# Attention weights of a two-layer graph network moved from SBUF to PSUM for VectorE's products

## The chip, the cores and the metric

The kernel runs on one core of one Trainium2 chip. The core has TensorE (PE in the profile, its weight loads PEld), VectorE (DVE), ScalarE (ACT), GpSimd (POOL) and SyncE (SP), which run beside each other and meet at semaphores; SBUF and PSUM are its on-chip memories, PSUM in 8 banks. The metric is the device time of one execution in microseconds: the median of the timed runs.

## The reference

Two graph layers run over x of shape (8, 2048, 256) with one adjacency matrix of 2048 x 2048, which has about 9 edges in a row. Layer 0 is chunked attention, layer 1 a graph attention with leaky-ReLU logits. Both end in a residual sum and a layer norm.

```
# layer 0: softmax within each chunk of 256 columns, masked entries count as score -10
q, k, v = heads(x @ Wq.T + bq), heads(x @ Wk.T + bk), heads(x @ Wv.T + bv)        # 4 heads of 64
scores = where(mask == 0, -10, clip(q.k / 8, -10, 10))                             # per chunk
ctx = sum over chunks of softmax(scores) @ v
x = layernorm(x + layernorm(ctx @ Wo.T + bo + x) * gamma + beta)              # eps 1e-5
# layer 1
Wh = x @ W
e = leaky_relu(s_src[i] + s_dst[j], 0.2), where adj, else -inf
x = layernorm(x + elu(softmax(e) @ Wh))
```

## The kernel before

The kernel works on edge lists rather than on dense matrices. A first part (`edge_lists`) reads the adjacency matrix, finds up to 24 neighbours of each row, and sorts the rows by how many they have, into 16 tiles of 128 rows; tile t takes `CAPS[t]` neighbour slots, 24 for the first and 5 for the last. A dense path exists for adjacency matrices that don't fit and isn't taken.

Layer 0 runs in 4 groups of 2 batches, so in 64 steps (g, t). The tables of keys and values (`kv_d`) and of queries and residuals (`qx_d`) of a group are written to DRAM by `tables`, one tile per step, one group ahead. A step then does the following. `fetch0` gathers, for each neighbour slot, 128 rows of `kv_d` with one indirect DMA on GpSimd's queue (L489) into a unit of two slots; the units come from a ring of 14 buffers. `scores0` multiplies keys by queries on VectorE (L547 into another buffer, L554 in place). For most units PE then transposes the products (L566), ScalarE copies them (`prT`, L572) and PE sums over the head's elements with a selection matrix (L576), so that the scores land in a PSUM bank; for the other units VectorE reduces (L556). `softmax0` reads the scores (L590) and makes the weights `al` (L596 to L607). `context0` multiplies the values by the weights: three quarters of the units on VectorE in one instruction each (`weighted`, L501, with the weights broadcast over 64 elements), the last quarter on ScalarE, 64 elements at a time (`weighted_act`, L507). PE transposes and accumulates the products in a bank "acc" (`summed`, L514). `finish0` is the output projection and both layer norms; `rows1` transposes its rows (`transposed`, L307), copies them (`x1T`, L658), projects them (L663) and writes the table `wh_d` of layer 1.

Layer 1 runs in 2 halves of 4 batches, so in 32 steps (p, t): `fetch1` gathers from `wh_d`, `softmax1` adds the logits (L680) and makes the weights `e` (to L700), `context1` multiplies and accumulates as in layer 0, `finish1` makes the norm, and scatters (L748, L753) put rows back in order through GpSimd's queue. The first half is interleaved with the layer-0 steps of groups 2 and 3; the second half runs alone at the end. Gathers are called one step ahead. On each engine the instructions stand in an order that the tile framework's scheduler made from the program's order; a buffer or bank is reused when its last reader is done.

PSUM has 8 banks: two each of "tf" (scores of layer 0 and the transposed rows of `rows1`), "tk" (the tables' transposes and projections), "acc", and one each of "mf" and "pr".

Of the kernel before, what the change touches and what calls it, by code (L numbers as in the profile page):

```python
# [14 lines left out]
ALU = mybir.AluOpType  # L15
AX = mybir.AxisListType

P = 128
# [16 lines left out]
TOP = 24  # L35
REC = 32
G = 2
UNIT = 2
# [135 lines left out]
def sparse_path(ctx: ExitStack, tc: tile.TileContext, keep, x, adj, Wq, bq, Wk, bk, Wv, bv, Wo, bo, gamma, beta, W, a,  # L174
                out):
    nc = tc.nc
# [5 lines left out]
    GF = G * F  # L182
    GH = G * H
# [46 lines left out]
    ps = ctx.enter_context(tc.tile_pool(name="ps", bufs=2, space=bass.MemoryType.PSUM))  # L230

    def bank(tag, bufs=2):

        return ps.tile([P, 512], F32, tag=tag, name=tag, bufs=bufs)

    with tc.tile_pool(name="prep", bufs=2) as prep:
        for dst, w, scale in ((wq, Wq, 0.125), (wkv[:, :, 0:F], Wk, 1.0), (wkv[:, :, F:], Wv, -1.0 / CH), (wo, Wo, 1.0)):
            wn = prep.tile([P, KC, F], F32, tag="wn", name="wn")
            nc.scalar.dma_start(wn, w.rearrange("(c p) f -> p c f", p=P))
            pt = bank("mf", 1).rearrange("p (c f) -> p c f", c=KC)  # L240
# [277 lines left out]
    got0, st0 = {}, {}  # L518
# [12 lines left out]
    def scores0(g, t):  # L531
        S = CAPS[t]
        qx, units = got0[g, t]
        q = qx[:, 0:GF]
        sc = small.tile([P, GH, S], F32, tag="sc", name="sc")

        npe = 1 + len(units) - len(units) // 3
        ps_sc = bank("tf")[:, 0:GH * S].rearrange("p (s e) -> p s e", e=GH)
        W8 = GH * DP
        qv = q.rearrange("p (k j w) -> p k j w", k=UNIT, w=W8).unsqueeze(3)  # L540

        def product(i):

            u, s0, n = units[i]
            room = units[i - 1][0][:, :, 0:GF]
            prod = room.rearrange("p k (j w) -> p k j w", w=UNIT * W8)[:, :, :, 0:n * W8]
            nc.vector.tensor_tensor(prod.rearrange("p k j (s w) -> p k j s w", w=W8),  # L547
                                    u[:, :, 0:GF].rearrange("p s (k j w) -> p k j s w", k=UNIT, w=W8),
                                    qv.to_broadcast([P, UNIT, NJ // UNIT, n, W8]), op=ALU.mult)
            return prod  # L550

        def reduced(u, s0, n):
            prod = u[:, :, 0:GF].rearrange("p s (j w) -> p s j w", w=W8)
            nc.vector.tensor_tensor(prod, prod, q.rearrange("p (j w) -> p j w", w=W8).unsqueeze(1)  # L554
                                    .to_broadcast([P, n, NJ, W8]), op=ALU.mult)
            nc.vector.tensor_reduce(sc[:, :, s0:s0 + n].rearrange("p e s -> p s e"),  # L556
                                    prod.rearrange("p s j (e d) -> p s e j d", d=DP),
                                    axis=AX.XY, op=ALU.add)
        reduced(*units[0])
        for i in range(1, npe, 4):  # L560
            some = units[i:min(i + 4, npe)]
            pr = bank("pr", 1).rearrange("p (k r) -> p k r", r=P)
            for k, (u, s0, n) in enumerate(some):
                prod = product(i + k)
                for j in range(NJ):
                    nc.tensor.matmul(pr[0:n * W8, k, :], prod[:, j // (NJ // UNIT), j % (NJ // UNIT), :], ident, is_transpose=True,  # L566
                                     start=(j == 0), stop=(j == NJ - 1), skip_group_check=True)
            m = len(some)
            prT = work.tile([P, 4, P], F32, tag="prT", name="prT", bufs=1)
            full = m - 1 if some[-1][2] < UNIT else m  # L570
            if full:
                nc.scalar.copy(prT[:, 0:full, :], pr[:, 0:full, :])  # L572
            if full < m:
                nc.scalar.copy(prT[0:W8, full, :], pr[0:W8, full, :])
            for k, (u, s0, n) in enumerate(some):
                nc.tensor.matmul(ps_sc[:, s0:s0 + n, :], prT[0:n * W8, k, :], sel[0:n * W8, 0:n * GH],  # L576
                                 start=(s0 == UNIT), stop=(k == m - 1 and i + m == npe), skip_group_check=True)
        for unit in units[npe:]:
            reduced(*unit)
        st0[g, t] = ps_sc, sc, min(S, UNIT * npe)  # L580


    ebuf = const.tile([P, GH * TOP + 1], F32, name="ebuf")
# [2 lines left out]
    def softmax0(g, t):  # L586
        S = CAPS[t]
        n = GH * S
        ps_sc, sc, sp = st0.pop((g, t))
        nc.vector.tensor_scalar(sc[:, :, UNIT:sp], ps_sc[:, UNIT:sp, :].rearrange("p s e -> p e s"), -10.0, 10.0, op0=ALU.max,  # L590
                                op1=ALU.min)
        for some in [sc[:, :, 0:UNIT]] + ([sc[:, :, sp:]] if sp < S else []):
            nc.vector.tensor_scalar(some, some, -10.0, 10.0, op0=ALU.max, op1=ALU.min)
        e = ebuf[:, 0:n]
        ev = e.rearrange("p (e s) -> p e s", s=S)
        nc.scalar.activation(ev, sc, AF.Exp)  # L596
        nc.vector.scalar_tensor_tensor(ev, ev, -EMIN, valid[:, t, 0:S].unsqueeze(1).to_broadcast([P, GH, S]),
                                       op0=ALU.add, op1=ALU.mult)

        al = small.tile([P, GH, S], F32, tag="al", name="al")  # L600
        z = al.rearrange("p e s -> p (e s)")
        nc.vector.tensor_tensor_scan(z, same[t][:, 0:n], e, 0.0, op0=ALU.mult, op1=ALU.add)
        zb = small.tile([P, n], F32, tag="zb", name="zb", bufs=1)
        nc.vector.tensor_tensor_scan(zb[:, ::-1], ebuf[:, n:0:-1], same[t][:, n:0:-1], 0.0, op0=ALU.add, op1=ALU.mult)
        nc.vector.scalar_tensor_tensor(z, z, CH * EMIN, zb, op0=ALU.add, op1=ALU.add)
        nc.vector.reciprocal(z, z)
        nc.vector.tensor_tensor(al, al, ev, op=ALU.mult)  # L607
        st0[g, t] = al

    def context0(g, t):  # L610
        S = CAPS[t]
        al = st0.pop((g, t))
        units = got0[g, t][1]
        acc = bank("acc").rearrange("p (c r) -> p c r", r=P)

        na = len(units) // 4
        if g == PG:
            places(t, units)
        for u, s0, n in units[len(units) - na:]:
            weighted_act(u[:, :, GF:2 * GF], al, s0, n)  # L620
        for i, (u, s0, n) in enumerate(units):
            if i < len(units) - na:
                weighted(u[:, :, GF:2 * GF], al, s0, n)
            summed(acc, u[:, :, GF:2 * GF], s0 == 0, s0 + n == S)
        cT = work.tile([P, G * KC, P], F32, tag="cT", name="cT", bufs=1)
        nc.scalar.copy(cT, acc)
        st0[g, t] = cT
# [25 lines left out]
    def rows1(g, t):  # L653

        o = st0.pop((g, t))
        pt = transposed(o.rearrange("p b f -> p (b f)"), "tf", 2)
        xT = work.tile([P, G * KC, P], F32, tag="x1T", name="x1T", bufs=1)
        nc.scalar.copy(xT, pt)  # L658
        wh = work.tile([P, WW], F32, tag="whs", name="whs")
        for b in range(G):  # L660
            pw = bank("mf", 1)
            for kc in range(KC):
                nc.tensor.matmul(pw[:, 0:F + 2 * H], xT[:, b * KC + kc, :], wa[:, kc, :], start=(kc == 0), stop=(kc == KC - 1))  # L663
            nc.scalar.copy(wh[:, b * F:(b + 1) * F], pw[:, 0:F])
            nc.scalar.copy(sd[g // 2 % 2][:, t, g % 2, b * H:(b + 1) * H], pw[:, F:F + H])
            nc.scalar.copy(wh[:, GF + b * H:GF + (b + 1) * H], pw[:, F + H:F + 2 * H])  # L666
        nc.sync.dma_start(wh_d[g // 2][t * P:(t + 1) * P, g % 2 * WW:(g % 2 + 1) * WW], wh)
# [7 lines left out]
    def softmax1(p, t):  # L675
# [21 lines left out]

        nc.vector.tensor_scalar(r, r, 1e-30, None, op0=ALU.max)
        nc.vector.reciprocal(r, r)
        nc.vector.tensor_tensor(e, e, r.unsqueeze(2).to_broadcast([P, 2 * GH, S]), op=ALU.mult)  # L700
        st1[p, t] = e

    def context1(p, t):
        S = CAPS[t]
        e = st1.pop((p, t))
        units = got1.pop((p, t))
        accs = [bank("acc").rearrange("p (c r) -> p c r", r=P) for _ in range(2)]
        na = len(units) // 4, (len(units) + 2) // 4
        for i, (u, s0, n) in enumerate(units):
            for k in range(2):  # L710
                if i >= len(units) - na[k]:
                    weighted_act(u[:, :, k * WW:k * WW + GF], e[:, k * GH:(k + 1) * GH], s0, n)
        for i, (u, s0, n) in enumerate(units):
            for k in range(2):
                part = u[:, :, k * WW:k * WW + GF]
                if i < len(units) - na[k]:
                    weighted(part, e[:, k * GH:(k + 1) * GH], s0, n)
                summed(accs[k], part, s0 == 0, s0 + n == S)
        hTs = []
        for k in range(2):  # L720
            hT = work.tile([P, G * KC, P], F32, tag="hT", name="hT")
            nc.scalar.copy(hT, accs[k])
            hTs.append(hT)
        xr = work.tile([P, 2, GF], F32, tag="xr", name="xr")
        nc.sync.dma_start(xr, x1_d[p][t * P:(t + 1) * P])
        st1[p, t] = hTs, xr
# [560 lines left out]
```

## Time and profile before

| | us |
|---|---|
| timed runs, median of 3 | 2586.16 (2584.35 to 2596.95) |
| profiled execution, its own time | 2397.55 |
| its span | 2395.8 |
| busy in the span: PE / DVE / POOL / ACT | 1900.4 / 1833.5 / 1505.0 / 1409.0 |
| 984 gathers L489: from kv_d, from wh_d (mean of one) | 810.2 (1.235), 416.5 (1.270) |
| 546 weighted products L501: layer 0, layer 1 (mean of one) | 334.5 (1.234), 314.4 (1.212) |

Busy time is what the engine spent in instructions; issuing and waiting don't count. A line of the groups view gives line, engine, operation, output and inputs with their shapes, the number of instructions, busy time and mean ns of one, and the idle time just before them with what ended it. In a waits view each line gives who waited for whom, the total, how many times, and the longest. The granted TensorE clock was 0.885 of full speed on the mean.

### The profile page before, as it was taken

Reading aid. Unit: us, or ns where it says so; the run is one execution under the profiler, and the core shown is the slowest. Engines: PE = TensorE matmul, PEld = TensorE weight load, DVE = VectorE, ACT = ScalarE, POOL = GpSimd, SP = SyncE. Lnnn points to the kernel's source line nnn. Section 1 sums busy time; section 2 is a strip of 40 time slices with the busy share of each in tenths; the row PEclk is TensorE's granted clock in tenths of the full one; section 3 lists DMA queues with packets and bytes.
Section 4 is the critical chain, followed back from the end, with each engine's and each line's share of the span. In section 5 each row is a group of like instructions: output and inputs, shape, how many; then the busy total and the mean of one; then the engine's idle time right before and its main releaser. Section 6 shows DMA issues by size and latency. Waiting matters only on the chain. (4 is left out here: it accounts for less than half of the span.)

```text
span 2395.8 us, 38844 instructions
## 1 busy us (share of the span) xinstructions
PE 1900.4 (79%) x11946; PEld 1622.0 (68%) x11946; DVE 1833.5 (77%) x4099; ACT 1409.0 (59%) x5036; POOL 1505.0 (63%) x1230
## 2 busy tenths in 40 slices
PE   7686889889899898999988885888678786664764
PEld 5565677778778787777876774776566675554653
DVE  6864587877588988588988886887788887775775
ACT  4573455546566555655565665664356677665766
POOL 3125455672666676376668856774677685787883
PEclk9897899899999999999998997987878987877887
DMA  7737877795889798598879977896679896786884
GB/s 259 242 137 272 265 270 281 260 346 209 316 287 320 260 334 319 212 388 298 302 258 353 360 281 238 285 321 221 230 274 326 306 319 248 278 310 231 302 296 154
DMA packets 239982, 669.10 MB, mean 279 GB/s; under 512 B 43688, under 2 KB 70059, under 8 KB 237719
## 3 DMA queue, kind: packets, MB, share of 16 engines
q0 software_dynamic: 156800, 505.01, 60.1%
q1 hardware_dynamic: 79248, 151.55, 17.2%
q10 hardware_dynamic: 3718, 9.97, 1.3%
q8 instruction: 98, 1.61, 0.3%
q14 instruction: 118, 0.96, 0.1%
HBM read 612.79 MB, written 126.36 MB: 309 GB/s over the span
## 5 line engine op out<-in xcount | busy, mean ns | idle before, releaser
L489 POOL DMA_INDIRECT u<-kv_d,idx x656 | 810.2, 1235 | 436.4 <-PE acc L514 185.7
L514 PE MATMUL acc<-ident,u 128*128 128x128 f32 x5248 | 713.4, 291 | 157.0 <-DVE u L501 89.0
L514 PEld LDWEIGHTS acc<-ident,u 128*128 128x128 f32 x5248 | 637.5, 151 | 220.7 <-DVE u L501 133.2
L489 POOL DMA_INDIRECT u<-wh_d,idx x328 | 416.5, 1270 | 148.2 <-issue 76.4
L566 PE MATMUL pr<-ident,u 128*128 128x128 f32 (+1 forms) x1984 | 287.0, 295 | 78.7 <-DVE u L547 77.2
L501 DVE TENSOR_TENSOR u<-u,al 128x1024 f32<-128x1024 f32 x280 | 334.5, 1234 | 1.5
L566 PEld LDWEIGHTS pr<-ident,u 128*128 128x128 f32 (+1 forms) x1984 | 245.4, 151 | 110.8 <-DVE u L547 104.6
L547 DVE TENSOR_TENSOR u<-u,qx 128x1024 f32<-128x1024 f32 (+1 forms) x248 | 302.0, 1218 | 18.3 <-DMA u<-kv_d,idx 15.1
L501 DVE TENSOR_TENSOR u<-u,z 128x1024 f32<-128x1024 f32 x266 | 314.4, 1212 | 0.6
L507 ACT ACTIVATE u<-u,z 128x64 f32<-128x64 f32 x1008 | 262.0, 337 | 25.0 <-DVE z L700 17.1
L507 ACT ACTIVATE u<-u,al 128x64 f32<-128x64 f32 x800 | 209.1, 342 | 23.2 <-DVE al L607 22.3
L663 PE MATMUL mf<-wa,x1T 128*128 128x264 f32 x512 | 167.6, 455 | 23.1 <-ACT x1T L658 14.8
L351 POOL TENSOR_TENSOR xt<-xt,beta_r 128x1024 f32<-128x1024 f32 x32 | 77.1, 2410 | 143.1 <-PE tk L336 126.3
L385 PE MATMUL tk<-wq,xT 128*128 128x256 f32 x512 | 145.2, 397 | 24.4 <-ACT kvs L379 24.4
L451 ACT ACTIVATE nm<-sums 128x2 f32<-128x2 f32 (+1 forms) x160 | 32.4, 202 | 221.3 <-DVE sums L641 122.6
L372 PE MATMUL tk<-wkv,xT 128*128 128x256 f32 x512 | 151.7, 410 | 12.9 <-ACT xC L341 12.6
L635 PE MATMUL mf<-wo,cT 128*128 128x256 f32 x512 | 148.4, 415 | 6.3 <-ACT whs L666 5.3
L376 PE MATMUL tk<-wkv,xC 128*128 128x256 f32 x512 | 144.5, 399 | 0.0
L663 PEld LDWEIGHTS mf<-wa,x1T 128*128 128x128 f32 x512 | 101.7, 218 | 59.7 <-ACT x1T L658 23.6
L455 ACT ACTIVATE sq<-o,nm 128x256 bf16<-128x256 f32 x256 | 129.7, 507 | 5.3
L554 DVE TENSOR_TENSOR u<-u,qx 128x1024 f32<-128x1024 f32 (+1 forms) x96 | 116.0, 1214 | 16.6 <-DMA qx<-qx_d,node 7.1
L590 DVE TENSOR_SCALAR sc<-tf 128x64 f32<-128x64 f32 (+5 forms) x64 | 14.0, 218 | 138.2 <-PE tf L576 138.2
(168 smaller groups left out, 3254.0 us busy)
## 6 DMA issues: line engine op xcount, KB each, us to landing
kv_d<-kvs SPq DMA_DIRECT2D x48, 512.0 KB, 6.0
wh_d<-whs SPq DMA_DIRECT2D x64, 260.0 KB, 5.8
xt<-in_x_dram SPq DMA_DIRECT2D x64, 256.0 KB, 4.8
qx_d<-xt SPq DMA_DIRECT2D x32, 512.0 KB, 4.4
qx_d<-qs SPq DMA_DIRECT2D x64, 256.0 KB, 5.8
x_d<-o SPq DMA_DIRECT2D x64, 256.0 KB, 5.2
xr<-x_d SPq DMA_DIRECT2D x32, 512.0 KB, 4.9
u<-kv_d,idx POOLq DMA_INDIRECT x656, 6.5
```

The lines of the kernel that those rows point to most:

```text
L372: nc.tensor.matmul(pm[:, 0:F], xT[:, b * KC + kc, rows], wkv[:, kc, 0:F], start=(kc == 0), stop=False, skip_group_check=True)
L376: nc.tensor.matmul(pm[:, F:], xC[:, b * KC + kc, rows], wkv[:, kc, F:], start=False, stop=(kc == KC - 1), skip_group_check=True)
L385: nc.tensor.matmul(qb, xT[:, b * KC + kc, rows], wq[:, kc, :], start=(b == 0 and kc == 0), stop=False, skip_group_check=True)
L455: nc.scalar.activation(sq, src[:, k, :], AF.Square, bias=nm[:, k:k + 1], accum_out=m2[:, k:k + 1])
L489: nc.gpsimd.indirect_dma_start(out=u[:, k, 0:width], out_offset=None, in_=table, in_offset=bass.IndirectOffsetOnAxis(ap=idx[:, t, s0 + k:s ...
L501: nc.vector.tensor_tensor(pv, pv, av, op=ALU.mult)
L507: nc.scalar.activation(pe, pe, AF.Copy, scale=al[:, e, s0 + k:s0 + k + 1])
L514: nc.tensor.matmul(acc[:, c, :], part[:, k, c * P:(c + 1) * P], ident, is_transpose=True, start=first and k == 0 and c == 0, stop=last and ...
L547: nc.vector.tensor_tensor(prod.rearrange("p k j (s w) -> p k j s w", w=W8), u[:, :, 0:GF].rearrange("p s (k j w) -> p k j s w", k=UNIT, w=W8),
L566: nc.tensor.matmul(pr[0:n * W8, k, :], prod[:, j // (NJ // UNIT), j % (NJ // UNIT), :], ident, is_transpose=True, start=(j == 0), stop=(j ...
L635: nc.tensor.matmul(po[:, b, :], cT[:, b * KC + kc, :], wo[:, kc, :], start=(b == 0 and kc == 0), stop=False, skip_group_check=True)
L663: nc.tensor.matmul(pw[:, 0:F + 2 * H], xT[:, b * KC + kc, :], wa[:, kc, :], start=(kc == 0), stop=(kc == KC - 1))
```

## The change

The weights that VectorE multiplies by now lie in PSUM. In layer 0 the score bank gets a tag of its own, "sc", with one buffer: columns up to 192 hold the scores, the columns behind them the weights `w`. In layer 1 the weights go to a bank "e1", with one buffer. ScalarE's products still read SBUF: for the units that it takes (the last quarter), a second, short product puts the weights into `al` or `e` as before. The bank "tf" is gone; the row transposes of `rows1` take their banks from "tk". The sum of banks stays 8. Products of keys and queries are as they were.

```diff
@@ scores0
-        ps_sc = bank("tf")[:, 0:GH * S].rearrange("p (s e) -> p s e", e=GH)
+        scb = bank("sc", 1)
+        ps_sc = scb[:, 0:GH * S].rearrange("p (s e) -> p s e", e=GH)
...
-        st0[g, t] = ps_sc, sc, min(S, UNIT * npe)
+        st0[g, t] = scb, sc, min(S, UNIT * npe)
@@ softmax0
-        ps_sc, sc, sp = st0.pop((g, t))
+        scb, sc, sp = st0.pop((g, t))
+        ps_sc = scb[:, 0:n].rearrange("p (s e) -> p s e", e=GH)
...
-        nc.vector.tensor_tensor(al, al, ev, op=ALU.mult)
-        st0[g, t] = al
+        w = scb[:, GH * TOP:GH * TOP + n].rearrange("p (e s) -> p e s", s=S)
+        nc.vector.tensor_tensor(w, al, ev, op=ALU.mult)
+
+        first = len(got0[g, t][1]) - len(got0[g, t][1]) // 4
+        if UNIT * first < S:
+            nc.vector.tensor_tensor(al[:, :, UNIT * first:], al[:, :, UNIT * first:], ev[:, :, UNIT * first:], op=ALU.mult)
+        st0[g, t] = w, al
@@ context0
-        al = st0.pop((g, t))
+        w, al = st0.pop((g, t))
...
-                weighted(u[:, :, GF:2 * GF], al, s0, n)
+                weighted(u[:, :, GF:2 * GF], w, s0, n)
@@ rows1
-        pt = transposed(o.rearrange("p b f -> p (b f)"), "tf", 2)
+        pt = transposed(o.rearrange("p b f -> p (b f)"), "tk", 2)
@@ softmax1
-        nc.vector.tensor_tensor(e, e, r.unsqueeze(2).to_broadcast([P, 2 * GH, S]), op=ALU.mult)
-        st1[p, t] = e
+        w = bank("e1", 1)[:, 0:2 * GH * S].rearrange("p (e s) -> p e s", s=S)
+        nc.vector.tensor_tensor(w, e, r.unsqueeze(2).to_broadcast([P, 2 * GH, S]), op=ALU.mult)
+        first = len(units) - (len(units) + 2) // 4
+        if UNIT * first < S:
+            nc.vector.tensor_tensor(e[:, :, UNIT * first:], e[:, :, UNIT * first:],
+                                    r.unsqueeze(2).to_broadcast([P, 2 * GH, S - UNIT * first]), op=ALU.mult)
+        st1[p, t] = w, e
@@ context1
-        e = st1.pop((p, t))
+        w, e = st1.pop((p, t))
...
-                    weighted(part, e[:, k * GH:(k + 1) * GH], s0, n)
+                    weighted(part, w[:, k * GH:(k + 1) * GH], s0, n)
```

## The prediction

> **What bounds the kernel now.** I read the page's busy table first, then busy time by stage, then what each engine waited for in each stage, then groups and timeline. The busy table alone names no bound:
>
> ```profile
> PE 1900.4 (79%) x11946; PEld 1622.0 (68%) x11946; DVE 1833.5 (77%) x4099; ACT 1409.0 (59%) x5036; POOL 1505.0 (63%) x1230
> ...
> 330.00:1100.00 770.00, 692.32 (x4427) 592.62 (x4426) 599.95 (x1196) 437.57 (x1677) 471.29 (x373) 0.95 0.82 293
> 1100.00:2010.00 910.00, 727.17 (x4721) 628.30 (x4719) 747.30 (x1612) 542.36 (x2000) 628.62 (x488) 0.87 0.82 289
> 2010.00:2396.00 386.00, 230.48 (x1557) 197.13 (x1555) 263.45 (x636) 257.57 (x906) 277.89 (x225) 0.80 0.73 266
> ```
>
> The last three lines are stages (length, then PE, PEld, DVE, ACT, POOL busy, granted clock, DMA share, GB/s). From 330 to 1100 us layer 0 runs alone, and PE is busy 90%. From 1100 to 2010 both layers interleave, and DVE leads (82%). From 2010 the second half of layer 1 runs alone (the tail). There POOL only looks 72% busy: each of its operations has some 0.30 us of issue time before it that isn't booked as busy (31.7 us over 104, below), 225 x 0.30 = 68 us, so it is taken 346 of 386 us. What ends waits in the tail agrees:
>
> ```profile
> DVE z L680 <- DMA u<-wh_d,idx: 63.6, 27, 5.0
> ...
> POOL u L489 <- issue: 31.7, 104, 0.3
> POOL out_dram L753 <- ACT xr L470: 27.9, 8, 13.4
> POOL u L489 <- PE acc L514: 6.4, 21, 0.3
> ```
>
> (us in total, times, longest.) DVE waits for gathers, while POOL waits hardly for ring buffers, only for its scatters' data (28 us). So **the tail is bound by POOL's issuing of gathers**; earlier stages aren't: in 330-1100 and 1100-2010 POOL itself waits 86.7 and 96.4 us for PE to free ring buffers.
>
> What sets the price of one gather is in the timeline:
>
> ```profile
> 1227.45 2.35 DVE L501 TENSOR_TENSOR u<-u,al 128x1024 f32<-128x1024 f32 x2
> ...
> 1227.66 1.89 POOL L489 DMA_INDIRECT u<-kv_d,idx  x1
> ...
> 1232.22 1.00 POOL L489 DMA_INDIRECT u<-kv_d,idx  x1 [0.30 <-PE acc L514]
> ```
>
> A gather issued while a weighted product (L501) runs takes 1.89 us, one that meets none 1.00. Sorted by the DVE instruction running at its start, the 984 gathers show: beside none 1.00 us (256 of them); beside the reduction L556, which reads one tensor, 1.00 (52); beside L641, whose one input is in PSUM, 1.00 (27); beside the products L501, L547, L554, which read two SBUF tensors, 1.69 (206), 1.44 (153), 1.47 (48).
>
> [...]
>
> ```profile
> L738 DVE SCALAR_TENSOR_TENSOR xr<-mf,xr 128x512 f32<-128x512 f32 x64 | 43.8, 684 | 21.5 <-ACT hT L737 9.9 <-DMA xr<-x_d 7.5 <-SPq L868 4.1
> L547 DVE TENSOR_TENSOR u<-u,qx 128x512 f32<-128x512 f32 x20 | 13.6, 679 | 0.1
> ```
>
> With one input in PSUM 684 ns, with both in SBUF 679. [...]
>
> **The change part by part**, against the profiled execution's own 2397.55 us (span 2395.8 and 1.8 around it). The median of the timed runs, 2586.16, is 189 us longer, for a reason that the profile doesn't show; I carry the sum over as microseconds, not as a share.
>
> *Weights read from PSUM (L501, 546 products).* Gathers beside them should fall to 1.00 us. Each indirect DMA's time above 0.995 us, shared out by overlap, sums to 277 us, of which beside L501: 2 us before 330, 21 in 330-1100, 67 in 1100-2010, 41 in the tail: 132 in all. L547 and L554 keep their share. What of it counts: in the tail POOL's 346 us becomes 305, but its scatters wait for ACT's rows, and these grow as POOL arrives earlier: between 20 and 41 us, I take 30. In 1100-2010 late gathers hold DVE 16.8 + 6.5 = 23 us, so up to 23; I take half, 12. In 330-1100 DVE waits 12 us for gathers and PE is full: 3. Sum -45, from -25 to -75. DVE gains too[...]: the 1024-element L501 means 1242 and 1216 ns (276 and 264 of them) against its undisturbed 1211, 10 us: -10.
>
> *Price of the PSUM operand.* By L738 at most 5 ns each, 3 us[...]. I take 0[...]. The writes of the weights (L607, L700) are as long as before. No row shows a DVE write into PSUM[...].
>
> *Copies of the tail weights for ACT.* 56 extra products in layer 0 (none where a step has three units), 32 in layer 1, 8 to 48 elements, by L680 and L698 (213 and 196 ns) 0.2 us each: 18 us of DVE. The 72 ahead of the tail, 14 us, lie where DVE is 78-82% busy: +11. ACT's products (L507) wait for them 0.2 us longer; ACT is 59% busy, so nothing, and without that cover 18 us more.
>
> *One bank "sc" for scores and weights.* PE may write step k+1's scores (L576) only when step k's last DVE product has read its weight. In the trace of before this always holds: over 63 steps the first score matmul starts 1.9 to 41 us after it. In the built program's PE order, too, they stand behind all of step k's accumulation matmuls (L514), in the changed kernel as in this one. 0; if that cover went, eight score matmuls (1.06 us) and a prT copy (0.58), some 1.6 us a step. Queued behind a waiting L576 on PE would be the table matmuls, and DVE's L590.
>
> *One bank "e1".* The next weights are written 1.1 us or more after the last product read the old ones, both on DVE: 0, either way.
>
> *Row transposes in the tables' banks.* They leave "tf" and become a fifth user per step of two "tk" banks (2 key/value, 1 query, 2 of x every second step). PE waits for tk evacuations today 24.4 (L385), 12.6 (L372) and 11.6 us (L336), 49 in all; a quarter more users, a quarter more: +12. Bounds -5 (the scores no longer share with the rows) and +69 (the rival below). Queued behind such a wait on PE are the products' transposes L566, hence L576 and DVE's L590. On POOL, add_beta (L351) waits for the x transposes and holds gathers; after 330 us that was 20 us, once. Neither SP's nor POOL's list of instructions changes in number.
>
> *Order.* The scheduler reshuffles DVE and PE: more of step k+1's products stand inside step k's softmax, more lies ahead of L590. That cuts L590's 138 us of waiting and delays weights: both signs, 0, with +-20.
>
> Sum: -45 - 10 + 11 + 12 = -32 us.
>
> **Rivals.** *Slower, the tk banks.* A row transposition holds a tk bank for four transposes (0.6 us) and the ACT copy (0.58 us), plus ACT's delay (22.4 us over 64, 0.35): 1.5 us. Tables and rows share the banks in about 46 steps up to 1425 us, where PE is 90% busy and waits for nothing cheaply: 69 us at most. From 44 us (two thirds exposed) on it eats the gain of 45 + 10 - 11. For it: the tk waits of up to 10.9 us at L385. Against: ACT is under 60% busy there. At its full price it gives -45 - 10 + 11 + 69 = +25, 2611.
>
> *Larger gain.* POOL's 132 us all count, because gathers that land earlier let the ring turn faster. For: POOL with its issue time is at 85% in 1100-2010. Against: there it waits 96 us for the ring. -132 - 10 + 11 + 12 = -119, 2467.
>
> *Nothing.* A gather is also held by something else (DMA at 0.82 busy)[...]: the tail keeps its time, within 13 us. Against: the 1.00 us beside L641 and only 0.73 DMA share in the tail.
>
> **How the numbers follow.** Forecast, -32: 2554 (own range 2525 to 2573), 0.45. Larger gain, 2467 (2445 to 2525): 0.15. Nothing, 2586 (2573 to 2599): 0.17. Slower, 2611 (2599 to 2645, with the reshuffle's 20 against it): 0.23. About 0.5%, 13 us, is what a measurement can tell from no change. So faster 0.60, same 0.17, slower 0.23. The range 2490 to 2615 leaves out some 0.09 of the larger gain and 0.10 of the slower case.
>
> **What would show it.** Gathers beside weighted products at 1.00 us, the mean of wh_d gathers from 1270 to about 1130 ns, kv_d from 1235 to about 1170; the tail from 386 to about 356 us; DVE's wait for gathers in the tail well under 64 us; 88 short products more; the weighted product still 1.21 us. Wrong if gathers beside them stay at 1.69 us[...],[...] if waits of tk or L590 grow by over 40 us (banks), or if gathers quicken and the tail does not (then POOL wasn't the bound).

## The result, and the profile after

The changed kernel takes **2713.73 us** (median of 4 runs, 2710.95 to 2725.14) beside 2585.26 us for the kernel before (4 runs, 2567.22 to 2596.95): a ratio of **1.0512** [1.0443, 1.058], slower by 128 us. The prediction was 2554 us, faster by 32.

The same kernel runs at two speeds, and a session (kernels run one after the other on one chip) is here wholly of one kind or the other. In three sessions the kernel before took 2384 to 2390 us; in two, and in the comparison above, 2532 to 2585. I call the first kind *quiet*, the second *late*. The profile of before, on which the prediction rests, was quiet (2397.55 us); the runs it was to predict were late. The profile of after is late (span 2713.8). A quiet profile of it, from the experiment g1_after_fourth, stands below. Medians are of all runs of a kernel; ratios leave out those over 1.5% above its fastest, so a ratio can differ from that of the medians (most in e7_l1_weights_tf).

The gathers in the groups of before, quiet, and then the busy table and groups of after, late (busy us, mean ns of one, idle before and its releaser):

```profile
L489 POOL DMA_INDIRECT u<-kv_d,idx x656 | 810.2, 1235 | 436.4 <-PE acc L514 185.7
...
L489 POOL DMA_INDIRECT u<-wh_d,idx x328 | 416.5, 1270 | 148.2 <-issue 76.4
```

```profile
PE 1983.0 (73%) x11946; PEld 1706.3 (63%) x11946; DVE 1816.2 (67%) x4187; ACT 1413.1 (52%) x5036; POOL 1324.7 (49%) x1230
...
L491 POOL DMA_INDIRECT u<-kv_d,idx x656 | 719.7, 1097 | 680.5 <-PE acc L516 403.7
...
L491 POOL DMA_INDIRECT u<-wh_d,idx x328 | 346.7, 1057 | 292.7 <-PE acc L516 144.7
...
L503 DVE TENSOR_TENSOR u<-u,sc 128x1024 f32<-128x1024 f32 x280 | 328.3, 1204 | 0.2
```

Everything that was to get cheaper did: POOL's busy time fell from 1505.0 to 1324.7 us, the means of the gathers (L489, now L491) from 1235 and 1270 to 1097 and 1057 ns, and the weighted product (L501, now L503) is no longer than before (1204 ns for 1234 in layer 0, 1206 for 1212 in layer 1). DVE's busy time is 17 us less, and PE does the same number of instructions. Yet the span grew by 318 us over the quiet profile of before. PE's busy time grew by 83 of them, with the lower granted clock (below); no other engine is busier by more than 5 us, so the rest is waiting. POOL now stands idle for PE to free ring buffers. From the waits of the same run (total, times, longest):

```profile
POOL u L491 <- PE acc L516: 548.4, 105, 19.3
...
DVE sc L594 <- PE sc L579: 181.7, 38, 12.2
...
ACT cT L635 <- remote: 90.3, 18, 20.1
...
DVE o L650 <- remote: 60.4, 3, 38.3
```

"remote" means that the trace has no semaphore event to name the releaser. As part of these events is missing in this trace (see below), the other names are less sure here than in a quiet one. One of these waits, in the timeline of after (start, duration, engine, line; in brackets the idle time before):

```profile
657.88 0.38 PE L315 MATMUL mf<-ident,bO 128*128 128x128 f32 x2
658.10 0.60 PE L378 MATMUL tk<-wkv,xC 128*128 128x256 f32 x2
...
670.24 0.42 DVE L650 CUSTOM_DVE_ANT_0 o<-mf,qx 128x256 f32<-128x256 f32 x1 [20.78 <-remote]
...
675.18 0.37 ACT L380 COPY kvs<-tk 128x256 f32<-128x256 f32 x1 [14.84 <-remote]
```

L650 reads the bank that L315 filled, L380 the one that L378 filled. By the records PE was done with both at 658.3 and 658.7 us, and started ten more matmuls in the 2 us after; the readers start at 670.24 and 675.18. The updates of PE's semaphore are recorded at 670.22 and 675.16. During the wait the DMA engines are full and PE, DVE and ACT stand still (windows of after: PE, PEld, DVE, ACT, POOL busy, granted clock, DMA share, GB/s):

```profile
650.00:660.00 10.00, 9.14 (x50) 7.68 (x51) 0.00 (x0) 5.43 (x23) 7.72 (x8) 1.00 0.91 291
660.00:670.00 10.00, 0.65 (x4) 0.22 (x2) 0.00 (x0) 0.19 (x1) 7.56 (x9) 0.71 1.02 395
```

In the quiet profile of before the stretch at the same group boundary has as full DMA engines, and no such stop:

```profile
620.00:630.00 10.00, 9.16 (x52) 7.53 (x52) 7.01 (x20) 4.86 (x20) 7.56 (x9) 1.00 1.02 389
630.00:640.00 10.00, 7.71 (x26) 6.45 (x27) 4.59 (x10) 4.09 (x15) 7.87 (x8) 0.66 1.03 411
```

The granted clock is lower in the late kind: 0.834 in this run against 0.897 in g1_after_fourth, 0.856 in e8_before_trace against 0.884 in e0_before_again. By the traces this follows the stops. They give the clock in pieces of 3.4 us, at full or at half speed. After a piece in which PE was busy under 40%, the next was at half speed each time in both kinds (84 of 84 in e0_before_again, 145 of 145 in after); after one busy over 90%, in 1 and in 3 of 100. A transpose (L516 in after, 128x128) took 273 ns at full and 421 at half speed (medians of 4458 and 790). PE's busy time is 126 us longer than in g1_after_fourth, so the half speed makes up at most a third of the 378 us between the two spans. Slower transfers aren't the reason either: the mean DMA packet took 124.3 ns in g1_after_fourth and 126.5 in after, 126.5 in e0_before_again and 127.9 in e8_before_trace.

The trace lists every recorded semaphore update with its time. In each quiet trace PE's update follows the end of the instruction by 0.014 us (over 99 of 100 within 0.02), and the numbers of updates and of signalling instructions agree (1816 and 1814 in e0_before_again). In each late trace about 1 in 9 of PE's updates, 1 in 4 of DVE's and ACT's and 4 in 10 of the DMA landings aren't recorded, and many of PE's that are come over 0.5 us after the latest PE instruction that could have caused them: in the changed kernel 155 stretches, together 396 us, the longest 22.7 us. DVE's recorded updates show nothing of the kind, ACT's little (28 us at most). I call the sum of these stretches (after 250 us) the **late sum**. It is 328 to 434 us in all nine late traces. In all eleven quiet ones it is 16 to 18 us, a single stretch. PE's ends are modelled, so this can't prove that the signal is late and not the matmul itself; that PE starts later matmuls within such a stretch, as above, speaks for the signal.

### The profile page after: what moved, and what is told of

It is laid out like the page before. It is cut to its first block, busy times and chain, and to the rows that moved or that the text cites. A ratio compares the mean times of both kernels' runs of the same rounds, so it can differ in the third digit from the quotient of the medians.

```text
span 2713.8 us, 38920 instructions
## 1 busy us (share of the span) xinstructions
PE 1983.0 (73%) x11946; PEld 1706.3 (63%) x11946; DVE 1816.2 (67%) x4187; ACT 1413.1 (52%) x5036; POOL 1324.7 (49%) x1230
## 5 line engine op out<-in xcount | busy, mean ns | idle before, releaser
L491 POOL DMA_INDIRECT u<-kv_d,idx x656 | 719.7, 1097 | 680.5 <-PE acc L516 403.7
L516 PE MATMUL acc<-ident,u 128*128 128x128 f32 x5248 | 726.8, 297 | 152.2 <-DVE u L503 72.1
L516 PEld LDWEIGHTS acc<-ident,u 128*128 128x128 f32 x5248 | 658.0, 155 | 206.5 <-DVE u L503 98.7
L491 POOL DMA_INDIRECT u<-wh_d,idx x328 | 346.7, 1057 | 292.7 <-PE acc L516 144.7
L503 DVE TENSOR_TENSOR u<-u,sc 128x1024 f32<-128x1024 f32 x280 | 328.3, 1204 | 0.2
L550 DVE TENSOR_TENSOR u<-u,qx 128x1024 f32<-128x1024 f32 (+1 forms) x248 | 296.0, 1193 | 27.1 <-DMA u<-kv_d,idx 22.7
L503 DVE TENSOR_TENSOR u<-u,e 128x1024 f32<-128x1024 f32 x266 | 313.2, 1206 | 0.0
L672 PE MATMUL mf<-wa,x1T 128*128 128x264 f32 x512 | 188.3, 499 | 79.5 <-issue 18.9
L650 DVE CUSTOM_DVE_ANT_0 o<-mf,qx 128x256 f32<-128x256 f32 x128 | 49.4, 420 | 168.0 <-PE mf L315 68.4
L387 PEld LDWEIGHTS tk<-wq,xT 128*128 128x128 f32 x512 | 96.7, 202 | 78.0 <-ACT kvs L381 51.5
L378 PE MATMUL tk<-wkv,xC 128*128 128x256 f32 x512 | 143.1, 393 | 0.0
L579 PE MATMUL sc<-sel,prT 128*128 128x16 f32 (+1 forms) x496 | 83.1, 293 | 74.9 <-ACT prT L575 41.1
```

Source lines behind the costliest of these rows:

```text
L378: nc.tensor.matmul(pm[:, F:], xC[:, b * KC + kc, rows], wkv[:, kc, F:], start=False, stop=(kc == KC - 1), skip_group_check=True)
L387: nc.tensor.matmul(qb, xT[:, b * KC + kc, rows], wq[:, kc, :], start=(b == 0 and kc == 0), stop=False, skip_group_check=True)
L491: nc.gpsimd.indirect_dma_start(out=u[:, k, 0:width], out_offset=None, in_=table, in_offset=bass.IndirectOffsetOnAxis(ap=idx[:, t, s0 + k:s ...
L503: nc.vector.tensor_tensor(pv, pv, av, op=ALU.mult)
L516: nc.tensor.matmul(acc[:, c, :], part[:, k, c * P:(c + 1) * P], ident, is_transpose=True, start=first and k == 0 and c == 0, stop=last and ...
```

## The experiments

The theories are named in each expectation; a letter holds within a session only. Stage times are read off the trace: a stage ends where ACT starts the last copy `cT` of a group of layer 0, or the last `hT` of layer 1. "tf kernel" is the change with weights in PSUM, but with all its banks under "tf".

### First session, quiet (kernel before: 2389.49 us)

**e0_before_again**: the kernel before, no edit.

> The kernel before, unchanged, to see how its profiled execution (2397.55 us) stands to its timed runs (median 2585 us). If the 2397 us were a rare execution, the new profile shows about 2580 us and the time is spread over the same waits that the changed kernel has; if the profiled state is real and the timed runs differ for another reason, the profile shows about 2400 us again. Ratio 1.00 in both cases.

Measured 2388.48 us, ratio 0.9991 [0.9968, 1.0014].

**e1_rows_tk**: the kernel before, and of the change only the banks of the row transposes.

```diff
-        pt = transposed(o.rearrange("p b f -> p (b f)"), "tf", 2)
+        pt = transposed(o.rearrange("p b f -> p (b f)"), "tk", 2)
```

> The kernel before with one part of the change: the row transposes take the tables' banks tk, scores keep two banks tf, all weights stay in SBUF. Theory A (the banks cost it: shared tk banks and the order they force): most of the 128 us, so 2650 to 2715 us, ratio 1.025 to 1.05. Theory B (the weights in PSUM cost it, by faster gathers that bunch up): 2575 to 2600 us, ratio 1.00.

2445.18 us, 1.0242 [1.0201, 1.0282]: **56 us slower**. ACT waits longer for what stands behind the rows in PE's order; in e0_before_again and in e1_rows_tk:

```profile
ACT prT L572 <- PE pr L566: 53.6, 32, 7.2
```

```profile
ACT prT L572 <- PE pr L566: 103.2, 39, 11.8
...
PE tk L307 <- ACT o L470: 63.8, 31, 6.3
```

PE stands at the rows' transposes (L307) until ACT has written `o`, 63.8 us in all, and the products' transposes (L566) stand behind. In the profile of before it was

```profile
PE tf L307 <- ACT o L470: 24.0, 11, 6.1
```

The two tk banks themselves aren't short: the waits for them that the prediction counted at 49 us (L385, L372, L336) are 36 in e1_rows_tk. What the edit changed is PE's order. In 31 of the 64 steps fewer of the products' transposes stand ahead of the rows than before; in 2 steps more do.

**e2_weights_tf**: the tf kernel. Against the changed kernel:

```diff
-        scb = bank("sc", 1)
+        scb = bank("tf")
-        pt = transposed(o.rearrange("p b f -> p (b f)"), "tk", 2)
+        pt = transposed(o.rearrange("p b f -> p (b f)"), "tf", 2)
-        w = bank("e1", 1)[:, 0:2 * GH * S].rearrange("p (e s) -> p e s", s=S)
+        w = bank("tf")[:, 0:2 * GH * S].rearrange("p (e s) -> p e s", s=S)
```

> The changed kernel with the old banks: scores and their weights in the two banks tf, the weights of layer 1 in a bank of tf too, the row transposes back in tf. All products of the weights still read PSUM. Theory A (banks): the gain that was forecast comes out, 2480 to 2575 us, ratio 0.96 to 0.995. Theory B (weights in PSUM): 2680 to 2720 us, ratio 1.04 to 1.05.

2345.11 us, 0.9822 [0.979, 0.9855]: **44 us faster**. In the quiet kind the weights in PSUM do what the prediction said (its terms -45, -10 and +11 sum to -44).

**e3_banks_only**: e1_rows_tk, and the scores in one bank of their own; weights stay in SBUF.

```diff
-        ps_sc = bank("tf")[:, 0:GH * S].rearrange("p (s e) -> p s e", e=GH)
+        ps_sc = bank("sc", 1)[:, 0:GH * S].rearrange("p (s e) -> p s e", e=GH)
```

> The kernel before with the banks of the change and nothing else: one score bank sc, row transposes in tk, all weights in SBUF as before, so no bank e1 and no extra copies. Theory A (banks): as slow as the changed kernel or slower, 2700 to 2760 us, ratio 1.045 to 1.07, since the gathers are held as before. Theory B (weights): about 2585 us, ratio 1.00. Less than the run with tk alone would put a part on the single score bank.

2440.51 us, 1.0244 [1.0195, 1.0293], as e1_rows_tk: one score bank in place of two costs nothing there, with no weights in it. Theory A had expected 1.045 at least.

### Second session, late (kernel before: 2531.95 us)

**e4_after_again**: the changed kernel, no edit.

> The changed kernel, unchanged, on a chip where the kernel before is measured beside it. Theory C (the parts add up, and the 5.1% on record belongs to a chip on which both kernels ran 190 us longer): where the kernel before takes 2389 us, weights give -44 and the shared tk banks +56, so about 2401 us, ratio 1.00 to 1.01. Theory D (the parts don't add up: faster gathers and shared banks hinder each other): ratio 1.05 again, 2510 us.

2648.75 us, 1.0455 [1.0395, 1.0514].

**e5_one_tf**: the changed kernel, with rows and layer-1 weights in one bank "tf", so that the rows leave "tk".

```diff
-        pt = transposed(o.rearrange("p b f -> p (b f)"), "tk", 2)
+        pt = transposed(o.rearrange("p b f -> p (b f)"), "tf", 1)
-        w = bank("e1", 1)[:, 0:2 * GH * S].rearrange("p (e s) -> p e s", s=S)
+        w = bank("tf", 1)[:, 0:2 * GH * S].rearrange("p (e s) -> p e s", s=S)
```

> The changed kernel with one edit taken back in part: the row transposes leave tk for a bank tf of their own with one buffer, which layer 1 uses for its weights too, in place of e1; the single score bank sc with the weights of layer 0 stays. Theory A (the tk banks alone cost it): as the run with all in tf, ratio 0.975 to 0.99, 2330 to 2365 us. If the single score bank or the single bank of layer-1 weights costs something in company with weights in PSUM: 1.00 or more.

2671.84 us, 1.0562 [1.0497, 1.0628]. Taking the rows out of "tk" at the price of one bank for them gains nothing.

**e6_l0_weights_tf** and **e7_l1_weights_tf**: the kernel before with the weights of one layer alone in PSUM, in "tf" (the change's lines for that layer, with `bank("tf")`), and that layer's 56 or 32 extra products.

> The kernel before with the weights of layer 0 alone in PSUM, behind the scores in the two banks tf, with the 56 extra short products; layer 1 as before. By the prediction's steps layer 0 saves what late gathers cost before 2010 us, 15, and pays 11: about 2385 us, ratio 0.99 to 1.005. The stages of the run with both layers (first two groups 21 us longer, tail 45 shorter) say 1.00 to 1.01.

> The kernel before with the weights of layer 1 alone in PSUM, in a bank of tf, with the 32 extra short products; layer 0 as before. The theory that the tail is bound by POOL's gathers: -30 to -50 us, nearly all in the stage after layer 0 has ended, so 2340 to 2360 us, ratio 0.98 to 0.988. If instead the gain of the run with both layers lies in the order that the scheduler makes: within 0.5% of the kernel before.

2620.12 us, 1.0331 [1.026, 1.0401], and 2592.8 us, 1.0161 [1.0071, 1.0251]. Both were expected lower (1.01 and 1.005 at most), by numbers of the quiet kind. Either layer's part, a gain together in the quiet kind, is a loss here, with the rows in "tf". So the rows in "tk" aren't needed for a loss in the late kind.

### Third session, late (kernel before: 2584.72 us)

**e8_before_trace** and **e9_after_third**: the kernels before and after, no edit. **e10_weights_tf_again**: the tf kernel.

> The kernel before, unchanged, for a trace of it on the same chip as the three kernels sent with it; both theories: ratio 1.00 within 0.005. If this chip is one where the kernel before takes about 2,530 us or more, theory A (signals between engines arrive late while gathers saturate the DMA engines) expects its trace to show stretches in which TensorE, VectorE and ScalarE all stand idle for over 1 us, in sum over 66 us, the sum of the trace of the kernel before that is at hand; theory B (the weights' place in PSUM or the order of work is slow by itself) expects 66 us within 10.

> The changed kernel, unchanged. On a chip where the kernel before takes about 2,390 us, both theories expect about 2,400 us: minus 44 for the weights in PSUM and plus 56 for the rows' transposes in the tables' banks, both measured on such a chip. On a chip where it takes 2,530 us or more: a ratio of 1.045 to 1.055, as in the two comparisons so far.

> The kernel with scores and weights in two banks that they share with the rows' transposes, which gained 44 us where the kernel before takes 2,390 us. On such a chip again: a ratio of 0.982 within 0.004. On a chip where the kernel before takes 2,530 us or more, theory A (late signals under saturated DMA engines) expects it slower than before, 1.02 to 1.05, since its gathers are as fast as those of the changed kernel; theory C (the rows' transposes in the tables' banks are what is slow in the changed kernel everywhere) expects 0.98 there too.

2591.19 us, 1.0037 [0.9999, 1.0076]; 2716.2 us, 1.0532 [1.0453, 1.061]; 2635.17 us, 1.0198 [1.0117, 1.028]. So the kernel of 0.9822 gives 1.0198 in the late kind. The late trace of the kernel before shows the stop without the change. In its windows PE, DVE and ACT do nothing in ten microseconds:

```profile
650.00:660.00 10.00, 2.21 (x10) 1.60 (x10) 0.97 (x2) 1.59 (x6) 7.63 (x8) 0.85 0.99 375
660.00:670.00 10.00, 4.63 (x12) 3.30 (x12) 3.88 (x11) 1.10 (x6) 7.86 (x8) 0.50 0.95 347
670.00:680.00 10.00, 0.00 (x0) 0.00 (x0) 0.00 (x0) 0.00 (x0) 7.18 (x8) 0.50 0.94 318
```

and in its timeline the copy that ends it waits 18.72 us. PE's last product for its bank (L376) ended at 653.38, and PE ran twelve later matmuls, for another copy, between 661.41 and 666.04:

```profile
652.35 1.03 PE L376 MATMUL tk<-wkv,xC 128*128 128x256 f32 x4
...
680.36 0.37 ACT L378 COPY kvs<-tk 128x256 f32<-128x256 f32 x1 [18.72 <-remote]
```

PE, DVE and ACT all idle for over 1 us: 146 us in this run, 68 in e0_before_again, as expected of late signals (over 66). Late sums: before 328, changed 410, tf kernel 419. In the kernel before, microseconds with the DMA engines over 95% busy are late to 20%, those under 80% to 6%; in the tf kernel 25% and 9%.

**e11_paced_tf**: the tf kernel, and after each gather a write of zeros on POOL.

```diff
                     bounds_check=N - 1, oob_is_err=False)
+                nc.gpsimd.memset(pad, 0.0)
```

> The kernel of e10_weights_tf_again with one write of zeros to 128x64 elements on GpSimd after each gather, about 0.15 us each (128x16 took 0.108 and 128x128 0.205 us), so that GpSimd gives out a gather every 1.25 us on average as in the kernel before, while the weights stay in PSUM. All 984 gathers get it, 148 us of GpSimd's time. On a chip where e10_weights_tf_again is slower than before, theory A (unbroken bursts of gathers delay the signals) expects the loss to go: a ratio at least 0.02 below that of e10_weights_tf_again. Theory B (the weights' place or the order of work) expects a ratio equal to it or above it. On a chip where e10_weights_tf_again gains, both expect that the gain shrinks to under a half, since its tail waits for GpSimd to give out gathers.

2715.91 us, 1.0522 [1.0441, 1.0603]: 81 us above e10_weights_tf_again, 41 of them before the first copy `cT`. The write took 153 ns; the late sum stayed, at 434. The theory expected a ratio lower by 0.02 at least, and fell: a slower mean pace of the gathers doesn't take the lateness away. (Where POOL has free buffers they still come without a pause.)

### Fourth session, quiet (kernel before: 2383.5 us)

**f1_half_before**, **f2_half_tf**, **f3_half_after**: the kernel before, the tf kernel and the changed one, with half of the table's rows left out of layer 0's gathers (group 1 stays whole).

```diff
-                    bounds_check=N - 1, oob_is_err=False)
+                    bounds_check=(N // 2 if width == 2 * GF else N) - 1, oob_is_err=False)
```

> The kernel before, with the bound of the first layer's gathers set to N // 2 instead of N for feature groups 0, 2 and 3, so that rows of the upper half of the table are not moved (about half of the bytes of these gathers; the tiles keep old data there). Same instructions, same waits. Group 1 and the second layer's gathers stay whole. On a chip where the kernel before takes 2,530 us or more, theory A (full DMA engines make TensorE's signals late) expects the late intervals (403 us long stage of group 0 among them) to shrink: stage of group 0 down from 403 to 380 us or less, and the sum of the intervals in which a TensorE update is over 0.5 us late, 340 us in the kernel before, to 220 us or less. Theory B (full DMA engines only stand beside it) expects the sum at 300 us or more.

> The kernel with scores, weights and rows in two banks (e10_weights_tf_again), with the same gathers cut as in f1_half_before. Where the kernel before takes 2,530 us or more, theory A expects the loss against its like to go: f2_half_tf minus f1_half_before between -45 and +10 us, where e10_weights_tf_again minus e8_before_trace was +44 us. Theory B (the weights in PSUM make the signals late whatever the DMA engines do) expects +30 us or more. Where the kernel before takes 2,390 us, both expect about -40 us.

> The changed kernel, with the same gathers cut as in f1_half_before. Theory A expects f3_half_after minus f1_half_before to be near the fast chip's sum, -44 and +56 us, so between 0 and +50 us, where the whole gathers gave +132 us. Theory B expects +90 us or more.

**f4_ring12_tf**: the tf kernel with `RING = 12` for 14.

> The kernel of e10_weights_tf_again with 12 units of gathered rows instead of 14, so 8 gathers fewer can be in flight. If the depth of what is in flight sets the lateness, the ratio to before falls below 1.0198 by 0.01 or more; if fullness of the DMA engines alone sets it, the ratio stays within 0.01 or rises, since GpSimd then waits longer for units.

The session was quiet, so these don't answer the question they were made for. In order: 2347.3 us, 0.9859 [0.9804, 0.9915]; 2288.59 us, 0.9601 [0.956, 0.9642]; 2321.06 us, 0.9735 [0.9692, 0.9778]; 2406.22 us, 1.0088 [1.0044, 1.0133]. The weights in PSUM gain 59 us here (f2 against f1), -40 expected; the changed kernel lies 26 us under f1 and 32 over f2, so its banks together cost 32. Two units of the ring are worth 61 us to the tf kernel (2406.22 against 2345.11 of e2_weights_tf, two sessions).

### Fifth session, quiet (kernel before: 2389.23 us)

**g1_after_fourth**: the changed kernel, no edit. **g2_half_tf_again**: f2_half_tf.

> The changed kernel, unchanged. Where the kernel before takes about 2,390 us: the sum of the two parts measured on such a chip, -44 us for the weights in PSUM and +56 us for the rows' transposes in the tables' banks, gives about 2,400 us, a ratio of 0.998 to 1.012. Where it takes 2,530 us or more: 1.045 to 1.055, as three times so far.

> The kernel with scores, weights and rows in two banks, and half of the gathered bytes left out in groups 0, 2 and 3 of the first layer (it leaves old rows in the tiles). Where the kernel before takes about 2,390 us: a ratio of 0.960 within 0.006, as in f2_half_tf. Where it takes 2,530 us or more: whole gathers gave 1.0198 there, and on the faster kind of chip the cut took 0.022 off the ratio (0.9822 to 0.9601). If full DMA engines make TensorE's signals late (theory A), the cut takes off more: a ratio of 0.975 or less, and a sum of the intervals with a late TensorE update of 280 us or less, where whole gathers gave 430 us. If they only stand beside it (theory B): a ratio of about 0.998, at least 0.988, and a sum of 380 us or more.

2346.79 us, **0.9823** [0.9795, 0.9851]: the changed kernel is **42 us faster in the quiet kind**. The sum of the two parts (+12) was wrong. 2291.71 us, 0.9581 [0.9551, 0.9611], as before. Busy table and groups of g1_after_fourth:

```profile
PE 1856.7 (80%) x11946; PEld 1610.2 (69%) x11946; DVE 1827.2 (78%) x4187; ACT 1404.5 (60%) x5036; POOL 1338.9 (57%) x1230
...
L491 POOL DMA_INDIRECT u<-kv_d,idx x656 | 733.2, 1118 | 464.4 <-PE acc L516 225.1
...
L491 POOL DMA_INDIRECT u<-wh_d,idx x328 | 347.2, 1058 | 185.2 <-PE acc L516 61.9
```

The durations are those of the late profile of after; POOL's idle time before the gathers of `kv_d` is 464.4 us instead of 680.5. The waits of its last 387 us, where before DVE waited 63.6 us for gathers:

```profile
POOL out_dram L767 <- ACT xr L472: 33.8, 14, 12.4
POOL u L491 <- issue: 31.4, 102, 0.6
...
DVE z L689 <- DMA u<-wh_d,idx: 21.7, 17, 3.0
```

Stages of the profiled runs, us:

| | start | group 0 | group 1 | group 2 | group 3 | tail | end |
|---|---|---|---|---|---|---|---|
| before, quiet (e0) | 246 | 377 | 379 | 456 | 489 | 426 | 24 |
| rows in tk, quiet (e1) | 245 | 379 | 406 | 463 | 502 | 420 | 24 |
| tf kernel, quiet (e2) | 245 | 381 | 398 | 450 | 462 | 381 | 24 |
| changed, quiet (g1) | 238 | 359 | 390 | 450 | 493 | 383 | 24 |
| before, late (e8) | 246 | 403 | 435 | 518 | 539 | 438 | 25 |
| tf kernel, late (e10) | 251 | 433 | 457 | 508 | 526 | 455 | 24 |
| changed, late (record) | 239 | 410 | 469 | 533 | 599 | 440 | 24 |

## Why the prediction was wrong

**The step that failed** is "I carry the sum over as microseconds, not as a share", of the 189 us by which the timed runs were longer than the profiled one "for a reason that the profile doesn't show". The step took these 189 us as the same for both kernels. They are not. Against the quiet kind the late one costs the kernel before 195 us (2389.23 to 2584.72, sessions 5 and 3), the tf kernel 290 (2345.11 to 2635.17) and the changed kernel 369 (2346.79 to 2716.2). The difference between the last and the first, 174 us, takes a gain of 42 to a loss of 132. No rival had it either: all were computed within the quiet profile. "Slower" had the sign, but from a price of the banks that the quiet kind doesn't show; of the 132 us lost in the third session, 50 come with the tf kernel and 81 more with the change's own banks. The gap of 8% between the profiled and the timed runs was in plain sight, and should have widened the range upwards.

**The quiet sum was nearly right**: -32 predicted, -42 measured (g1_after_fourth). By its terms:

- *Gathers at 1.00 us*: right. In g1_after_fourth the 277 that start beside a weighted product take 1.00 us on the mean (206 at 1.69 before). The time above 0.995 us fell from 277 to 111 us, by 166 where 132 were expected. The 132 were too small because the excess was shared by overlap with all of VectorE's instructions, also those that don't hold a gather up (12 us went to L556, beside which a gather takes 1.00); shared among L501, L547 and L554 alone, the trace of before has 160 us beside L501, 52 of them in the tail where the prediction had 41.
- *Tail, -30 (20 to 41)*: -43 in the stages (426 to 383), a little outside; the quiet tf kernel gives -45. POOL's issuing was the bound, and when it got shorter DVE's wait for gathers fell to a third (63.6 to 21.7 us). Which wait comes next was right too: the scatters wait for ACT's rows (33.8 us).
- *Price of the PSUM operand, 0*: right, 1204 ns in both kinds (1234 before, from SBUF). *DVE*: -7.5 us on the products (641.4 for 648.9), predicted -10; 88 short products more, as counted.
- *One bank "sc", 0*: right in the quiet kind for scores alone (e3_banks_only beside e1_rows_tk); with the weights in it no run separates it from the other banks.
- *Rows in "tk", +12*: wrong in its mechanism too. The sum had a quarter more users wait a quarter longer for banks; those waits fell (49 us to 36 in e1_rows_tk), and PE waited for ACT's rows instead. It isn't one number either. Alone the edit costs 56 us (e1_rows_tk); with weights in PSUM the change's banks together cost 32 with half the gathers (f3 less f2) and about 0 with whole ones (0.9823 and 0.9822, two sessions): group 3 is 31 us longer than in the tf kernel, group 0 is 22 shorter. The rival's place was right (PE's transposes queued behind), its price of up to 69 near for the edit alone, but it was worked out from how long banks are held, so the nearness is luck. Why the edit pays so differently is open.
- *Order, 0 +-20*: it is through PE's order that the rows in "tk" act, as the waits of e1_rows_tk say; 56 us is more than the 20 allowed. Other effects of the order aren't separated.

**What the late kind does to it.** Shown: the program and PE's order are the same in both kinds (g1_after_fourth and after), and so are the busy times but for PE's; PE's completions are recorded late in the late kind, and in no quiet trace; each layer's weights lose by themselves (e6, e7), and the change's banks add to it (tf kernel 1.0198, changed 1.0532). In the third session the late sum is greater with weights in PSUM (410 and 419) than without (328), but that is one trace of each; the second session has 348 for the changed kernel and 340 and 333 for one layer's weights. In the tail the changed kernel's gain is gone: 440 us against 438.

Argued, not shown: a late completion costs more where less slack is left. The changed kernel has one bank for scores, one for layer-1 weights, and rows queued ahead of tables on PE, so each late completion holds more engines. The late sums of the changed and the tf kernel are alike (410, 419) while their times differ by 81 us, which fits.

Open: what makes a session late; whether full DMA engines have a part in the late completions or only stand beside them (f1 to f3 and g2 met quiet sessions; alone they aren't enough, as they are as full in the quiet profile); whether weights in PSUM raise the late sum, and why. The sessions' chip number doesn't settle it: number 4 stands at a late session (the second) and at a quiet one (the fifth), so it may be a state that changes in time. The late traces have both stalls and missing updates (396 us of late stretches and about 1 in 9 of PE's updates in after), but no run shows that the one causes the other. Every timed run on record comes with a span and a granted clock, and the profiled run is one of them, so no run tells what the kernels take when nothing is recorded.

Of the versions that ran in both kinds none beats the kernel before in both. The tf kernel gains the same in the quiet kind (0.9822) and loses less in the late one (1.0198) than the changed kernel (1.0532).

## What to carry to other kernels

Before a sum made on a profile is carried to timed runs, make the two agree: here the profiled execution was 7% shorter than the median, the profile was of another regime, and a change that gained 42 us in it lost 132 in the other. An operand moved to PSUM did free GpSimd's issue of gathers from VectorE's products (beside them 1.69 us before, 1.00 after), and that gain could be counted, gather by gather, where GpSimd was the bound. Moving a consumer to banks that another chain uses must be judged by what then stands behind it in PE's order, not by the count of users alone: the rows' move cost 56 us by itself, and with the change's other banks and weights in PSUM 32 or about 0.

## What the runs showed of the hardware

A kernel can run at two speeds (the kernel before 6 to 8% apart, the changed one 13 to 16%) with nearly equal busy times: DVE's, ACT's and POOL's busy times agree within 3% between e0_before_again and e8_before_trace, and PE's is 3.5% longer, at a lower granted clock (0.856 against 0.884). What differs is when PE's completions are recorded and the others go on: 0.014 us after the modelled end in the quiet kind, up to 22.8 us in the late one (e9_after_third). In e8_before_trace two thirds of that time lie in microseconds with the DMA engines over 95% busy. The granted clock was at half speed after each 3.4 us piece with PE busy under 40%, in both kinds (84 of 84 in e0_before_again, 145 of 145 in after). And GpSimd's gathers beside a product with one input in PSUM took 1.00 us, beside one with both inputs in SBUF 1.48 (277 gathers beside L503 and 130 beside L550 in g1_after_fourth).
